# Expert slots of a two-layer block: the down product one slot later, the up weights in halves

## The chip, the cores and the metric

One NeuronCore of a Trainium2 chip runs the whole program. The metric is the device time of one execution in microseconds (us), as the median of several runs. PE is TensorE (PEld its weight loads), DVE VectorE, ACT ScalarE, POOL GpSimd, and SP the engine from whose queue most DMA transfers are issued. Each engine works through its own list of instructions in order and waits on semaphores of the others; while it waits, nothing behind the waiting instruction on that list can start.

## The reference

Two layers, each an attention block and a feed-forward block with gated residuals, on x of 4 x 512 x 512 in float32. The change lies in the first layer's feed-forward block, a mixture of 8 experts in which each token takes two, beside a shared expert. Cut to that:

```python
scores = softmax(xf @ gate_w)
_, sel = top_k(scores + expert_bias, 2)            # two experts for each of 2048 tokens
order = argsort(sel.reshape(-1), stable=True)      # rows sorted by expert
routed_in = xf[order // 2] * top_scores_sorted[:, None]
h = silu(ragged_dot(routed_in, w1, counts)) * ragged_dot(routed_in, w3, counts)
routed_out = ragged_dot(h, w2, counts)
out = silu(xf @ sw1) * (xf @ sw3) @ sw2
out = out.at[order // 2].add(routed_out)
```

An expert has 512 inputs, 448 hidden units and 512 outputs. The layer that follows is an attention with two sources of keys and a feed-forward block whose weights are rounded to three values.

## The kernel before

The parts of the block run one after the other, and each part prepares weights for a later one beside its own work. `moe` is the first layer's feed-forward block. It normalises the tokens, chooses the experts, scatters the scaled rows to a DRAM buffer of 39 slots of 128 rows each (`SLOTS`), runs the shared expert, and then loops over the slots. The rows of one slot belong to one expert, whose number is read from a small table by SP (`values_load`).

For each slot there are these steps.
- `load` reads the expert's number and sends for the up weights (`w13`, 1792 KB, two buffers that alternate). It is skipped on the chip where the expert is the one of two slots before.
- `load_rows` fetches the slot's 128 rows from ACT's queue, four slots ahead.
- `turn_in` (L861) transposes the rows in four 128 x 128 pieces on PE and copies them from PSUM to SBUF.
- `up` (L870) makes both up products in float32, `pu` and `pw`, over four chunks of the 512 inputs. ACT takes SiLU of `pu` (L874), DVE multiplies by `pw` (L875).
- `turn_hidden` (L881) transposes the hidden units in four pieces and copies them.
- `down` (L888) makes the down product. ACT scales it (L893) and its queue stores it in a second DRAM buffer.
- `load_down` (L855) sends for the down weights (`w2`, 896 KB, two buffers), skipped as `load` is.

The copies (`evac`, L120 on DVE and L122 on ACT) alternate between the two engines. SP's queue also carries two kinds of preparation in this loop. `split` holds the steps that split the second layer's weights in two halves of lower precision: a fetch (L1147), for some a scaling and a centring on DVE (L1137, L1115 to L1117), a cast on ACT (L1141), a subtraction on POOL (L1142) and a store (L1143) of 512 KB. There are 80 of them. `ternary` holds the steps that sum and then code the last block's weights: a fetch of 704 KB (L1890), DVE work (a sum, L1897, or three passes, L1920 to L1922), and for the coding a store (L1923).

The order of instructions on an engine isn't that of the source. A scheduler with a cost model chooses it from the dependences. Where `tc.keep_in_program_order` records an instruction (class `Ordered`), its order on the engine is the one in which the program emits it. In the slot loop before, nothing is recorded so. PE's list is up(s), hidden(s-1), in(s+1), down(s-1) for the middle slots, with some groups split or exchanged, and up(s), hidden(s), in(s+2), down(s) from slot 26 on.

After the loop the same function goes on to the keys and values of the second layer's context, 64 units of one product (`m_pk`) each, on PE in program order.

Of the kernel before, what the change touches and what calls it, by code (L numbers as in the profile page):

```python
# [22 lines left out]
P = 128  # L23
# [4 lines left out]
KC = D // P  # L28
# [5 lines left out]
E, HID, HC = 8, 448, 112  # L34
NHC = HID // HC
SLOTS = (2 * T + E * (P - 1)) // P
# [561 lines left out]
def moe(k, split, codes8, scratch, ffn):  # L598
# [11 lines left out]
    nc, tc, a = k.nc, k.tc, k.a  # L610
    with ExitStack() as ctx:
# [12 lines left out]
        w13 = [  # L624
            p1.tile([P, KC, 2, HID], F32, tag=f"m_w13_{j}", name=f"m_w13_{j}") for j in range(2)
        ]
# [38 lines left out]
        for b in range(B):  # L665
            k.layernorm([(xn[b][:, t, :], k.x[:, b * TB + t, :]) for t in range(TB)])
            for c in range(KC):
                pt = ps_m.tile([P, S], F32, tag="ps_m")
# [44 lines left out]
        def by_token(name):  # L713
            return p1.tile([P, NT], F32, name=name)
# [34 lines left out]
        pt = ps_m.tile([P, 2, NT, E], F32, tag="ps_m", name="r_counts")  # L749
# [41 lines left out]
        for r, hot in enumerate(hots):  # L791
# [8 lines left out]
            s = by_token(f"r_s{r}")  # L800
# [22 lines left out]
        got = {}  # L823

        def load(s):


            e = got["e", s] = nc.values_load(
                owners[:, s : s + 1], engines=(mybir.EngineType.SP,), min_val=0, max_val=E - 1,
                skip_runtime_bounds_check_because="it is at most E - 1 by construction",  # L830
            )
            got["new", s] = None if s < 2 else e != got["e", s - 2]
            nc.sync.dma_start(w13[s % 2], a["w13"][e], cond=got["new", s])

        def load_rows(s):
            work = p6.tile([P, 4, D], F32, tag="m_big", name=f"m_work{s}")
            rows = nc.scalar.dma_start(work[:, 0, :], rows_in[ts(s, P), :])
            for scatter in scatters:
                tc.add_manual_dep(
                    rows.ins, scatter.name,  # L840
                    mybir.DependencyInfo(mybir.DependencyClass.Sync, mybir.DependencyReason.DATA),
                    reason="any of them may write a row of the slot",
                )

            tc.add_manual_dep(
                rows.ins, silus[B * NHC - NHC - 1].name,
                mybir.DependencyInfo(
                    mybir.DependencyClass.NoSync, mybir.DependencyReason.SCHED_ONLY
                ),
                reason="order of ScalarE's queue",  # L850
            )
            got["work", s] = work

        def load_down(s):
            nc.sync.dma_start(w2[s % 2], a["w2"][got["e", s]], cond=got["new", s])  # L855

        def turn_in(s):
            work = got["work", s]
            pt = ps_m.tile([P, KC, P], F32, tag="ps_m")
            for c in range(KC):  # L860
                nc.tensor.transpose(pt[:, c, :], work[:, 0, ts(c, P)], k.ident)  # L861
            k.evac(work[:, 1, :].rearrange("p (c t) -> p c t", c=KC), pt)

        def up(s):
            work, w = got["work", s], w13[s % 2]
            pu = ps_h.tile([P, HID], F32, tag="ps_h")
            pw = ps_h.tile([P, HID], F32, tag="ps_h")
            for c in range(KC):
                for half, pp in enumerate((pu, pw)):
                    nc.tensor.matmul(  # L870
                        pp, lhsT=work[:, 1, ts(c, P)], rhs=w[:, c, half, :],
                        start=(c == 0), stop=(c == KC - 1),
                    )
            nc.scalar.activation(work[:, 2, 0:HID], pu, AF.Silu)  # L874
            nc.vector.tensor_tensor(work[:, 2, 0:HID], work[:, 2, 0:HID], pw, ALU.mult)  # L875

        def turn_hidden(s):
            work = got["work", s]
            pt = ps_m.tile([P, NHC, P], F32, tag="ps_m")
            for m in range(NHC):  # L880
                nc.tensor.transpose(pt[:HC, m, :], work[:, 2, ts(m, HC)], k.ident)  # L881
            k.evac(work[:HC, 3, :].rearrange("p (c t) -> p c t", c=NHC), pt[:HC])

        def down(s):
            work, w = got.pop(("work", s)), w2[s % 2]
            po = ps_o.tile([P, D], F32, tag="ps_o")
            for m in range(NHC):
                nc.tensor.matmul(  # L888
                    po, lhsT=work[:HC, 3, ts(m, P)], rhs=w[:, m, :],
                    start=(m == 0), stop=(m == NHC - 1),  # L890
                )
            y = p4.tile([P, D], F32, tag="m_row", name=f"m_y{s}")
            nc.scalar.activation(y, po, AF.Copy, scale=k.tg[:, 2:3])  # L893
            nc.scalar.dma_start(rows_out[ts(s, P), :], y)
# [3 lines left out]
        def load_weights(i):  # L898
            ws[i] = p6.tile([P, KC, 512], F32, tag="m_big", name=f"m_wx{i}")
            nc.sync.dma_start(ws[i], a["w_kvx"][i])  # L900

        def load_context(b):
            ctxT.append(p6.tile([P, KC, S], F32, tag="m_big", name=f"m_ctxT{b}"))
            nc.sync.dma_start(
                ctxT[b], a["ctxT"][:, ts(b, S)].rearrange("(c p) t -> p c t", p=P)
            )
# [4 lines left out]
        for s in range(2):  # L911
            load(s)
            load_down(s)
        turn_in(0)
        up(0)
        turn_in(1)
        for s in range(SLOTS):
            if s + 1 < SLOTS:
                up(s + 1)
            turn_hidden(s)  # L920
            if s + 2 < SLOTS:
                load(s + 2)
                turn_in(s + 2)
            down(s)
            if s + 2 < SLOTS:
                load_down(s + 2)
            if s + 4 < SLOTS:
                load_rows(s + 4)
            for _ in range(-(-len(split) // (SLOTS - s))):
                split.pop(0)(ps)  # L930
            if ternary:
                ternary.pop(0)()
            if s == SLOTS - 4:
                load_weights(0)
                load_context(0)
            elif s == SLOTS - 2:
                for c in range(KC):
                    centred(k, ws[0][:, c, 0:256], 2)


        kaff = p1.tile([P, 2], F32, name="kx_affine")
# [5 lines left out]
        VE, AE, GE, PE = (Ordered(tc, e) for e in (nc.vector, nc.scalar, nc.gpsimd, nc.tensor))  # L947
# [97 lines left out]
        got = {}  # L1045
# [54 lines left out]
        for c in range(KC):  # L1100
            m = 20 + 9 * c
# [8 lines left out]
def centred(k, w, heads):  # L1110

    nc = k.nc
    wv = w.rearrange("p (h d) -> p h d", d=D1)
    m = k.small.tile([P, heads], F32, tag="s_mean")
    nc.vector.tensor_reduce(m, wv, AX.X, ALU.add)  # L1115
    nc.vector.tensor_scalar(m, m, -1.0 / D1, None, ALU.mult)
    nc.vector.tensor_tensor(wv, wv, m[:, :, None].to_broadcast([P, heads, D1]), ALU.add)  # L1117
# [819 lines left out]
@with_exitstack  # L1937
def kernel(ctx: ExitStack, tc: tile.TileContext, a: dict, out: bass.AP):
    k = Kernel(ctx, tc, a, out)
    xattn_int8(k)  # L1940
    scratch, split = split_weights(k)
    with tc.tile_pool(name="codes", bufs=1) as pool:
        codes8 = Codes(k, pool)
        ffn = Ffn(k)
        first = moe(k, split, codes8, scratch, ffn)
        attend_and_feed(k, scratch, codes8, first, ffn)
# [85 lines left out]
```

## Time and profile before

| | us |
|---|---|
| median of 3 runs | 3576.08 (3575.98 to 3579.71) |
| the profiled execution | 3574.1 |
| its span | 3572.4 |
| slot stage, from its first transpose to the first m_pk | 869.14 to 1315.50 |

The profile comes from one execution, and a span in it begins with the first instruction. A row of the timeline gives start, duration, engine, line, what is written from what, and in brackets how long the engine stood idle before it and which instruction or transfer ended that. A matmul of float32 shows as two records. [...] L567 is the helper that records order, so many groups of later stages share that line.

### The profile page before, as it was taken

The numbers are of one execution on the slowest core, as the hardware profiler recorded it, in microseconds if no ns is written. First come the engines' busy times: TensorE is split into PE (matmuls) and PEld (weight loads), VectorE is DVE, ScalarE is ACT, GpSimd is POOL, SyncE is SP. The second block draws the span as 40 slices with busy tenths as digits, with TensorE's granted clock in tenths as the row PEclk, the third lists the DMA queues.
The fourth block names the chain that finished last, engine by engine and source line by source line (L and its number), as shares of the span: only waits on it lengthen the run. The fifth ranks groups of instructions, "written<-read, shape, count | busy, mean of one in ns | idle before, by whom it ended". The sixth has DMA issues, their size and how long they took to land.

```text
span 3572.4 us, 47015 instructions
## 1 busy us (share of the span) xinstructions
PE 3333.4 (93%) x15536; PEld 2190.3 (61%) x15552; DVE 2172.4 (61%) x4580; ACT 1544.1 (43%) x4456; POOL 1355.3 (38%) x1526
## 2 busy tenths in 40 slices
PE   6988987889999889989999999999999999999997
PEld 3544544534554444447777777776777777777775
DVE  6676767543133336525558766678766687676657
ACT  2544545111211223345554455554555554555543
POOL 1000000341000134624446654557545466544443
PEclk8999999899999999989999999999999999999998
DMA  5534441476354673552323233223332332333211
GB/s 183 156 98 130 121 101 41 167 254 234 104 198 151 225 257 128 177 174 72 115 98 107 101 115 110 95 99 108 109 125 92 118 107 77 128 105 111 83 60 36
DMA packets 223026, 452.86 MB, mean 127 GB/s; under 512 B 21440, under 2 KB 80320, under 8 KB 220224
## 3 DMA queue, kind: packets, MB, share of 16 engines
q1 hardware_dynamic: 206432, 412.62, 35.2%
q10 hardware_dynamic: 11232, 20.45, 1.7%
q0 software_dynamic: 5120, 16.78, 1.4%
q8 instruction: 125, 2.05, 0.2%
q14 instruction: 117, 0.96, 0.1%
HBM read 420.87 MB, written 116.98 MB: 151 GB/s over the span
## 4 chain that ended last, share of the span: by engine, by line
PE 73%; DVE 13%; DMA 4%; ACT 4%; POOL 3%; issue 3%; SPq 0%; DVEq 0%; POOLq 0%; ACTq 0%
PE ps_w L567 10%; PE pss L567 10%; PE ps_p L567 9%; PE ps_o L567 9%; PE ps_t L567 7%; PE m_pk L567 5%; PE po L888 3%; PE pu L870 3%; PE pw L870 3%; PE po L468 3%; PE pt L460 3%; DVE f_y L567 2%; PE pss L438 2%; PE pk L403 2%; PE pv L373 2%
## 5 line engine op out<-in xcount | busy, mean ns | idle before, releaser
L567 PEld LDWEIGHTS ps_w<-g_pT,g_v 128*128 128x128 f32 x2048 | 388.8, 191 | 299.7 <-issue 223.1
L567 ACT ACTIVATE g_p<-pss,nm 128x512 f32<-128x512 f32 x512 | 350.9, 685 | 479.7 <-DVE nm L567 436.4
L567 PE MATMUL ps_w<-g_pT,g_v 128*128 128x256 f32 x2048 | 530.4, 382 | 24.1 <-DVE f_y L567 13.7
L567 PE MATMUL pss<-g_kT,g_qT 128*128 128x512 f32 x1024 | 524.1, 594 | 0.9 <-ACT g_p L567 0.9
L567 POOL TENSOR_SCALAR g_p<-g_p,rs 128x512 f32<-128x512 f32 x512 | 368.4, 721 | 382.1 <-DVE rs L567 370.6
L567 DVE TENSOR_REDUCE nm<-pss 128x1 f32<-128x512 f32 x512 | 350.9, 685 | 102.7 <-PE pss L567 101.7
L567 PE MATMUL ps_t<-ident,g_p 128*128 128x128 f32 x2048 | 307.5, 273 | 0.0
L1142 POOL TENSOR_TENSOR hl<-raw,hl 128x512 fp32r<-128x512 f32 x80 | 102.0, 1282 | 519.2 <-ACT hl L1141 503.1
L567 POOL TENSOR_TENSOR g_rstd<-ss,neghalf 128x4 f32<-128x4 f32 (+1 forms) x192 | 185.0, 964 | 297.5 <-ACT ss L567 297.3
L567 PE MATMUL ps_p<-g_wq,g_xq 128*128 128x512 f32 x1024 | 282.3, 417 | 5.3 <-DMA g_wq<-s_q 4.9
L567 PE MATMUL ps_o<-g_wp,g_cq 128*128 128x512 f32 x1024 | 287.0, 423 | 0.0
L567 DVE COPY g_pT<-ps_t 128x512 f32<-128x512 f32 x244 | 167.1, 685 | 165.8 <-PE ps_t L567 165.4
L567 POOL TENSOR_TENSOR f_t<-f_y,f_c 128x512 f32<-128x512 bf16 (+1 forms) x180 | 206.6, 1148 | 155.4 <-DVE f_c L567 87.1
L567 PEld LDWEIGHTS ps_t<-ident,g_p 128*128 128x128 f32 x2048 | 243.8, 141 | 26.3 <-POOL g_p L567 1.1
L567 ACT COPY g_pT<-ps_t 128x512 f32<-128x512 f32 x268 | 156.1, 583 | 233.4 <-PE ps_t L567 233.4
L446 ACT ACTIVATE p<-pss,nm 128x512 f32<-128x512 f32 x256 | 175.3, 690 | 135.9 <-DVE nm L443 134.5
L567 PE MATMUL m_pk<-m_wx,m_ctxT 128*128 128x512 f32 x512 | 230.0, 592 | 0.0
L567 PEld LDWEIGHTS ps_o<-g_wp,g_cq 128*128 128x128 f32 x1024 | 196.7, 192 | 41.4
L567 PEld LDWEIGHTS ps_p<-g_wq,g_xq 128*128 128x128 f32 x1024 | 191.4, 190 | 48.9 <-issue 7.1
L443 DVE TENSOR_REDUCE nm<-pss 128x1 f32<-128x512 f32 x256 | 173.2, 687 | 70.7 <-PE pss L438 69.3
L567 ACT ACTIVATE junk<-ps_p 128x128 f32<-128x128 f32 x640 | 177.1, 277 | 68.5 <-PE ps_p L567 54.2
L567 DVE RECIPROCAL rs<-g_sm 128x1 f32<-128x1 f32 x512 | 82.5, 161 | 203.3 <-ACT g_p L567 201.4
(317 smaller groups left out, 6025.4 us busy)
## 6 DMA issues: line engine op xcount, KB each, us to landing
m_w<-in_w_dram SPq DMA_DIRECT2D x39, 1792.0 KB
g_wp<-s_proj SPq DMA_DIRECT2D x128, 512.0 KB
m_w<-in_w_dram SPq DMA_DIRECT2D x39, 896.0 KB
g_wq<-s_q SPq DMA_DIRECT2D x128, 256.0 KB
g_wq<-s_qx SPq DMA_DIRECT2D x128, 256.0 KB
st_k<-dhl_k SPq DMA_DIRECT2D x64, 256.0 KB
st_q<-dhl_q SPq DMA_DIRECT2D x64, 256.0 KB
s_proj<-hl SPq DMA_DIRECT2D x32, 512.0 KB
```

What stands on the lines that cost most here:

```text
L373: nc.tensor.matmul(pv, lhsT=ctxT[:, ic, ts(t, P)], rhs=wkvT[:, ic, D : 2 * D], start=(ic == 0), stop=(ic == KC - 1),)
L403: nc.tensor.matmul(pk, lhsT=wkvT[:, ic, ts(oc, P)], rhs=ctxT[:, ic, :], start=(ic == 0), stop=(ic == KC - 1),)
L438: nc.tensor.matmul(pss, lhsT=qk["q"][:, h, ts(qt, P)], rhs=qk["k"][:, h, :], start=True, stop=True,)
L443: nc.vector.tensor_reduce(nm, pss, AX.X, ALU.max, negate=True)
L446: nc.scalar.activation(p, pss, AF.Exp, bias=nm, accum_out=sums[:, qt, n : n + 1])
L460: nc.tensor.transpose(pt[:, c, :], p[:, ts(c, P)], k.ident)
L468: nc.tensor.matmul(po[ts(h, DH0)], lhsT=v[:, c, ts(oc * 4 + h, DH0)], rhs=pTs[h][:, c, :], start=(c == 0), stop=(c == TB - 1),)
L567: return lambda *args, **kw: self.tc.keep_in_program_order(call(*args, **kw))
L870: nc.tensor.matmul(pp, lhsT=work[:, 1, ts(c, P)], rhs=w[:, c, half, :], start=(c == 0), stop=(c == KC - 1),)
L888: nc.tensor.matmul(po, lhsT=work[:HC, 3, ts(m, P)], rhs=w[:, m, :], start=(m == 0), stop=(m == NHC - 1),)
L1142: nc.gpsimd.tensor_tensor(hl[:, 1, :], raw, hl[:, 0, :].bitcast(F32), ALU.subtract)
```

## The change

Four things change in the slot loop. PE's instructions are recorded in program order. The down product of a slot moves behind the up product of the slot after next in the emitted order: an iteration emits up(s+1), hidden(s), in(s+2), down(s-1), and the last down product follows the loop. The up weights come in two transfers of 896 KB, each with the same condition, and `load(s+3)` is emitted straight after `up(s+1)`, where `load(s+2)` stood after `turn_hidden(s)`. `load_down(s+1)` follows `down(s-1)`. The splitting steps are spread over the first 34 slots: 3 a slot for 12 slots and then 2, where they were 3 for two slots and then 2 to the end.

```diff
@@ load @@
-            nc.sync.dma_start(w13[s % 2], a["w13"][e], cond=got["new", s])
+            for c in (0, KC // 2):
+                some = slice(c, c + KC // 2)
+                nc.sync.dma_start(w13[s % 2][:, some], a["w13"][e][:, some], cond=got["new", s])
...
+        PE = Ordered(tc, nc.tensor)
+
         def turn_in(s):
...
-                nc.tensor.transpose(pt[:, c, :], work[:, 0, ts(c, P)], k.ident)
+                PE.transpose(pt[:, c, :], work[:, 0, ts(c, P)], k.ident)
...
@@ up, turn_hidden and down: nc.tensor becomes PE in the same way @@
...
         turn_in(0)
         up(0)
+        load(2)
         turn_in(1)
         for s in range(SLOTS):
+
             if s + 1 < SLOTS:
                 up(s + 1)
+            if s + 3 < SLOTS:
+                load(s + 3)
             turn_hidden(s)
             if s + 2 < SLOTS:
-                load(s + 2)
                 turn_in(s + 2)
-            down(s)
-            if s + 2 < SLOTS:
-                load_down(s + 2)
+            if s:
+                down(s - 1)
+                if s + 1 < SLOTS:
+                    load_down(s + 1)
             if s + 4 < SLOTS:
                 load_rows(s + 4)
-            for _ in range(-(-len(split) // (SLOTS - s))):
+            for _ in range(-(-len(split) // max(1, SLOTS - 5 - s))):
                 split.pop(0)(ps)
...
+        down(SLOTS - 1)
```

More of the change, by code (lines that the diff above doesn't have):

```diff
@@ L869, in up @@
                 for half, pp in enumerate((pu, pw)):
-                    nc.tensor.matmul(
+                    PE.matmul(
                         pp, lhsT=work[:, 1, ts(c, P)], rhs=w[:, c, half, :],
@@ L880, in turn_hidden @@
             for m in range(NHC):
-                nc.tensor.transpose(pt[:HC, m, :], work[:, 2, ts(m, HC)], k.ident)
+                PE.transpose(pt[:HC, m, :], work[:, 2, ts(m, HC)], k.ident)
             k.evac(work[:HC, 3, :].rearrange("p (c t) -> p c t", c=NHC), pt[:HC])
@@ L887, in down @@
             for m in range(NHC):
-                nc.tensor.matmul(
+                PE.matmul(
                     po, lhsT=work[:HC, 3, ts(m, P)], rhs=w[:, m, :],
```

## The prediction

> **What bounds the kernel now.** I read the page first, then the windows of the slot stage, then the waits of the weight-load side of TensorE (PEld), and last the order of time around three slots. The profiled execution took 3574.1 us (span 3572.4), 2.0 below the median of the three runs, 3576.1; I make the sum on its trace and subtract it from the median.
>
> ```profile
> PE 3333.4 (93%) x15536; PEld 2190.3 (61%) x15552; DVE 2172.4 (61%) x4580; ACT 1544.1 (43%) x4456; POOL 1355.3 (38%) x1526
> ```
>
> TensorE is the bound. Only time in which it idles, or runs slowly after idling, can be won. The change touches the 39 slots of the expert stage. There the windows (length, then busy time and count of PE, PEld, DVE, ACT, POOL, then clock, DMA share, GB/s) show a full PE first, and idle later:
>
> ```profile
> 1050.00:1100.00 50.00, 48.76 (x151) 25.03 (x150) 19.02 (x26) 8.80 (x15) 1.27 (x1) 1.00 0.58 191
> 1150.00:1200.00 50.00, 45.44 (x135) 22.33 (x134) 15.57 (x25) 12.39 (x21) 10.07 (x8) 1.00 0.63 222
> 1200.00:1250.00 50.00, 42.62 (x123) 20.58 (x122) 17.23 (x31) 10.44 (x18) 7.61 (x6) 0.97 0.65 226
> 1250.00:1320.00 70.00, 61.16 (x167) 28.82 (x166) 22.95 (x51) 16.68 (x29) 17.69 (x14) 0.98 0.70 248
> ```
>
> In the waits of PEld from 1130 to 1320 us (total, times, longest), the hidden transposes wait for DVE's product, the down product waits for ACT's copy, and few waits are for weights:
>
> ```profile
> PEld pt L881 <- DVE m_work L875: 21.5, 14, 2.7
> PEld po L888 <- ACT m_work L122: 8.3, 13, 1.6
> PEld pu L870 <- DMA m_w<-in_w_dram: 6.1, 3, 2.9
> ```
>
> The timeline of one late slot shows why. Its up product is followed at once by its own transposes and its own down product, so PE stands still twice:
>
> ```profile
> 1192.42 0.54 ACT L874 ACTIVATE m_work<-pu 128x448 f32<-128x448 f32 x1 [4.58 <-PE pu L870]
> ...
> 1193.24 0.62 DVE L875 TENSOR_TENSOR m_work<-m_work,pw 128x448 f32<-128x448 f32 x1 [9.33 <-PE pw L870]
> ...
> 1193.92 0.65 PE L881 MATMUL pt<-ident,m_work 128*112 128x128 f32 x4 [0.79 <-DVE m_work L875]
> ...
> 1195.24 3.70 PE L888 MATMUL po<-m_w,m_work 112*128 112x512 f32 x8 [0.24 <-ACT m_work L122]
> ```
>
> **The stage counted.** From the timeline of PE: an up product takes 6.02 us (16 records, start to start of what follows), a down product 3.43, a group of four transposes 0.44. A slot without waits is 6.02 + 3.43 + 2 x 0.44 = 10.33, and 39 slots are 402.9. The stage runs from the first transpose (869.14) to the first matmul of the next stage (m_pk, 1315.50): 446.4. So 43.5 us are lost. The starts of the up products say where. Slot 2 (887.37) to 24 (1124.21) is 10.77 a slot, a loss of 22 x 0.44 = 9.6. Slot 24 to 38 (1300.61) is 12.60 a slot; taking off one down product and one group of transposes that move into this stretch (3.87), 27.9 are lost. The rest, 6.0, lies at the two ends (2.0 of it is the last down product, which after a stand took 5.40). In the quiet late slots the period is 11.82, so 1.49 each is the two stands above; slots 33 and 34, whose experts are new, lose 2.2 and 4.3 more.
>
> **The change part by part.**
> *Down one slot later, PE in program order.* No instruction is added on PE, DVE or ACT. The instruction order of the changed kernel, built but not run, is up(s+1), hidden(s), in(s+2), down(s-1) for every slot. The hidden transposes have a whole up product (6.02) to cover DVE's product (0.62 and two hand-overs), the down product's copy is a slot old, and the down product (3.43) covers the copy of in(s+2) (0.69). DVE's order puts product and copy first and the splitting after them in nearly every slot. So the 43.5 can go. If the cover fails (a splitting step that waits for its DMA ahead of a copy on DVE), PE now cannot take other work, and the delay is paid whole.
>
> *The head keeps a loss.* Slots 0 to 2 have no down product between in and up. up0 waits 0.84 as now. up1 waits behind product (0.62) and copy (0.69) plus hand-overs, about 1.4. Before up2 DVE also has the sum over a w_dn piece (1.62 by its row): about 2.6. Together 4.9.
>
> *Up weights in halves, sent ahead.* The splits' stores wait on POOL in SP's queue, and whatever is behind them waits too. Here are the issues around the load of slot 33 in SP's timeline, and under them the PE row that waited for it:
>
> ```profile
> 1226.04 0.09 SPq L855 DMA_DIRECT2D m_w<-in_w_dram  x1
> 1226.24 0.84 SPq L1147 DMA_DIRECT2D raw<-in_w_q_dram  x2
> 1228.05 0.35 SPq L833 DMA_DIRECT2D m_w<-in_w_dram  x1
> ...
> 1236.45 1.02 PE L870 MATMUL pu<-m_w,m_work 128*128 128x448 f32 x2 [2.03 <-DMA m_w<-in_w_dram]
> ```
>
> Issues of 0.33 us and more move data, those of 0.1 are skipped; by that, slots 16, 17, 18, 33 and 34 fetch, and landing took 8.4 to 10.9 us. By the program, load(s+3) may go at the end of up(s+1), 2 x 4.31 + 6.02 = 14.6 before up(s+3): enough for 16 to 18. But in SP's new order the stores of a splitting step stand ahead of load 33, and two more between the halves of load 34. Load 33: product and copy (2.2 with hand-overs), 3.5 us of DVE, cast and two POOL operations (0.62 + 2 x 1.27) and the issues between put it about 9.7 after up31 ends. I let the first half land 5.5 later and the second 10, at 15.2 and 19.7; they are wanted at 14.6 and 17.6, so 0.6 and then about 1.8 is lost. Load 34: its second half goes out behind stores that wait for casts placed after slot 33's SiLU, some 17.7 after up32 ends; with 1 MB of stores before it it lands 7 later, at 25, and is wanted at 20 (up34 then begins at 17): 5 lost. The 896 KB down loads of 33 and 34, also behind stores, may miss by 1 each (896 KB took 6.27: 1239.83 to 1246.10). Together 9.4 stay, somewhat more than the 6.5 that these slots lose now.
>
> Each half adds one issue and its register work on SP, some 0.2 us, 39 times: nothing on the path while SP waits for others (by SP's waits L855 alone waits 151.5 us for PE). Two fetches issued together at 1166.88 were used by ACT at 1169.78 in two casts with no gap between (1.27 for both), so a second landing of the same queue costs next to nothing here. [...]
>
> *Splitting over 34 slots.* The same steps, none added; the last five slots are free of them. In slots 20 to 29 two steps meet one coding step of the feed-forward weights. There one turn of SP is: issue two fetches and the piece (1.3), landing 5.5 (1167.76 to 1173.30), three DVE passes 2.8, store 0.4: 10.0 against PE's 10.33, so it keeps up barely; I take 2 us of stalls (0 to 10). Another 2 for slots 14 to 18, where DVE has seven passes ahead of a product.
>
> *Sum.* 43.5 - 4.9 - 9.4 - 2 - 2 = 25.2 us. The next stage is PE without gaps (3.65 us a unit), so what comes early stays early. 3576.1 - 25 = 3551.
>
> **The rivals.**
> *Slower: SP's turn becomes the period.* Two such turns in the trace, from L855 to L855, took 14.24 and 15.62:
>
> ```profile
> 1136.88 0.09 SPq L855 DMA_DIRECT2D m_w<-in_w_dram  x1
> ...
> 1151.12 0.10 SPq L855 DMA_DIRECT2D m_w<-in_w_dram  x1
> ...
> 1161.80 2.85 SPq L1143 DMA_DIRECT2D s_kv<-hl  x2
> 1166.00 0.32 SPq L1923 DMA_DIRECT2D ffn_codes<-t_raw  x1
> 1166.74 0.09 SPq L855 DMA_DIRECT2D m_w<-in_w_dram  x1
> ```
>
> With half b of the up load behind the store of codes, PE would then wait each time. Ten slots at 14.93 cost 46 where I put 2: 3551 + 44 = 3595. It ends slower once a turn is over 10.33 + (25.2 + 2) / 10 = 13.05 in those ten. Against it: the issue at 1151.12 waited for a down product that ended at 1151.18 by its row, and the 15.62 had DVE idle 6.98 for PE's product first. These were PE's pace; the new DVE order takes that away.
>
> *Little gain.* PE keeps its order but is stopped about 0.35 a slot by late copies (39 x 0.35 = 13.7): gain 12, 3564. For it: the strict order; against: DVE is busy 15 to 20 of 50.
>
> *Nearly all.* The stores are earlier than I reckon, both loads are covered and SP keeps ahead: only the head and 3 us stay, 36 won, 3540. "Sent ahead" not doing what it says (loads still behind stores) is inside my forecast, not a rival.
>
> Order before the stage also shifts slightly (DVE held PE 6.41 at 855.20 in the shared part): plus or minus 4 on all.
>
> **How the numbers follow.** 0.2%, 7 us, is about what a measurement here can tell from no change. Forecast (gain 17 to 32): 0.56. Little gain (7 to 17): 0.17. Nearly all (over 32): 0.13. Within 7: 0.08, where two of the costs add up. Slower, almost all SP's turn: 0.06. So faster 0.86. The range 3540 to 3567 (gain 9 to 36) takes in the rivals' own values and the 4 us of the rule.
>
> **What would show it.** Right: PE's waits for the product and for the copy of the hidden units gone, a period near 10.3 in most slots, m_pk starting about 25 earlier with respect to the first transpose, waits for weights only at 33 and 34 (5 to 10 together). Wrong: up products of slots 20 to 29 waiting for a skipped load (SP behind), or copies of in(s+2) late in most slots; or the stage shorter but the next one starting later for want of ctxT or centred weights, both sent only after down product 34, 28 us before their use.

## The result, and the profile after

The changed kernel takes 3561.33 us (median of 5 runs, 3556.91 to 3564.90); the kernel before, run beside it, 3576.08 (5 runs, 3572.80 to 3579.71). The ratio is 0.996 with a 95% interval of 0.9949 to 0.9971: 14.8 us are won, between 10 and 18. I forecast 25 (3551) with a range of 3540 to 3567. The profiled execution took 3561.25 us (span 3559.5), 12.9 less span than before.

The page's first line, to be read against the one shown before, has TensorE still fullest by far, 10.1 us less busy for the same 15536 matmuls.

```profile
PE 3323.3 (93%) x15536; PEld 2189.1 (61%) x15552; DVE 2170.0 (61%) x4580; ACT 1544.1 (43%) x4456; POOL 1356.3 (38%) x1526
```

The windows of the slot stage (length, busy time and count of PE, PEld, DVE, ACT, POOL, then clock, DMA share, GB/s) show where the gain is, and where it stops:

```profile
1050.00:1100.00 50.00, 50.00 (x157) 26.11 (x156) 23.39 (x44) 12.43 (x21) 7.81 (x6) 1.00 0.62 207
1100.00:1150.00 50.00, 48.11 (x150) 24.46 (x149) 18.00 (x21) 12.73 (x22) 12.57 (x9) 1.00 0.68 241
1150.00:1200.00 50.00, 47.32 (x140) 23.91 (x139) 31.22 (x49) 11.99 (x20) 9.25 (x7) 0.97 0.61 207
1200.00:1250.00 50.00, 39.39 (x103) 19.19 (x102) 9.83 (x27) 9.57 (x17) 10.12 (x8) 0.87 0.69 242
1250.00:1320.00 70.00, 68.57 (x201) 33.96 (x200) 11.27 (x26) 18.40 (x45) 11.61 (x11) 1.00 0.61 214
```

From 1050 to 1100 us TensorE has no gap (48.76 of 50 busy before). From 1200 to 1250 it is worse than before: 39.39 busy against 42.62, at a clock of 0.87 against 0.97. TensorE's waits from 862 to 1320 us (total, times, longest) say what for:

```profile
PE pu L567 <- DMA m_w<-in_w_dram: 12.3, 6, 5.4
PE po L567 <- DMA m_w<-in_w_dram: 4.2, 4, 2.4
PE pu L567 <- issue: 2.1, 1, 2.1
PE pu L567 <- DVE m_work L120: 0.9, 1, 0.9
PE pu L567 <- ACT m_work L122: 0.7, 1, 0.7
```

The waits for the product (L879) and for the hidden copy are gone. In their place 16.5 us of waits for weights stand (5.8 before). ("Issue" is a wait for which the profile names no cause; it stands before up product 2.) In the sync queue, SP's, the lines of the changed kernel are L857 for the down loads, L835 for the up loads, L1156 for the fetches of splitting, L1152 for its stores and L1932 for the store of codes. Over the same stretch the stores of the split halves wait for GpSimd:

```profile
SPq L1152 <- POOL hl L1151: 128.3, 38, 11.5
```

Before they waited 153.8, so the waiting itself is not new; what is new is the pace that TensorE asks of the queue behind it. One turn of that queue, from one down load to the next (1103.35 to 1120.38), took 17.03 us:

```profile
1103.35 0.09 SPq L857 DMA_DIRECT2D m_w<-in_w_dram  x1
1103.49 0.83 SPq L1156 DMA_DIRECT2D raw<-in_w_proj_dram  x2
...
1116.12 2.20 SPq L1152 DMA_DIRECT2D s_proj<-hl  x2
1118.75 0.32 SPq L1932 DMA_DIRECT2D ffn_codes<-t_raw  x1
1119.85 0.09 SPq L835 DMA_DIRECT2D m_w<-in_w_dram  x1
1120.38 0.09 SPq L857 DMA_DIRECT2D m_w<-in_w_dram  x1
```

The two stores stand in the queue ahead of an up load's half and the next down load. What they wait for is in the rows of ScalarE and GpSimd:

```profile
1111.79 0.54 ACT L878 ACTIVATE m_work<-pu 128x448 f32<-128x448 f32 x1 [4.58 <-PE pu L567]
1112.98 0.59 ACT L122 COPY m_work<-pt 112x512 f32<-112x512 f32 x1 [0.65 <-PE pt L567]
1113.46 1.14 ACT L1150 CAST hl<-raw 128x512 fp32r<-128x512 f32 x2
...
1114.16 3.81 POOL L1151 TENSOR_TENSOR hl<-raw,hl 128x512 fp32r<-128x512 f32 x2 [12.56 <-ACT hl L1150]
```

The casts stand in ScalarE's order behind the SiLU of the slot, which itself waits for TensorE, and so the stores go out only when the next up product is over. From 1075.55 to 1226.86 the queue made 12 such turns in 151.3 us, 12.6 each, while TensorE needs 10.33. By the down load issued at 1203.54, whose buffer was free at 1186.19, it was 17.4 us behind. At slot 33, whose expert is new, TensorE pays:

```profile
1214.51 0.09 SPq L857 DMA_DIRECT2D m_w<-in_w_dram  x1
1214.70 1.59 SPq L1156 DMA_DIRECT2D raw<-in_w_kv_dram  x2
1217.16 1.12 SPq L835 DMA_DIRECT2D m_w<-in_w_dram  x2
```

```profile
1214.63 3.70 PE L567 MATMUL po<-m_w,m_work 112*128 112x512 f32 x8 [0.38 <-DMA m_w<-in_w_dram]
1223.69 1.83 PE L567 MATMUL pu<-m_w,m_work 128*128 128x448 f32 x2 [5.36 <-DMA m_w<-in_w_dram]
1225.31 1.70 PE L567 MATMUL pw<-m_w,m_work 128*128 128x448 f32 x2
...
1229.79 0.94 PE L567 MATMUL pu<-m_w,m_work 128*128 128x448 f32 x2
...
1245.15 1.86 PE L567 MATMUL pu<-m_w,m_work 128*128 128x448 f32 x2 [4.78 <-DMA m_w<-in_w_dram]
```

Both halves of load 33 were issued together, 14.6 us after up product 31 ended (1202.5), and landed in some 6.5. After the stand the first pairs of matmuls take 1.5 to 1.6 us, start to start, where a running TensorE takes 0.75 (its records, 0.92 long, overlap); the granted clock in the trace is 0.5 from 1223.00 to 1229.83. The second stand, at 1245.15, is the second half of load 34, which had been issued at 1237.89 behind two more stores.

### The profile page after: what moved, and what is told of

Read it like the earlier page. It is cut to its first block, busy times and chain, and to the rows that moved or that the text cites. A ratio compares the mean times of both kernels' runs of the same rounds, so it can differ in the third digit from the quotient of the medians.

```text
span 3559.5 us, 47228 instructions
## 1 busy us (share of the span) xinstructions
PE 3323.3 (93%) x15536; PEld 2189.1 (61%) x15552; DVE 2170.0 (61%) x4580; ACT 1544.1 (43%) x4456; POOL 1356.3 (38%) x1526
## 4 chain that ended last, share of the span: by engine, by line
PE 46%; DVE 7%; POOL 1%; ACT 1%; issue 1%; DVEq 0%; POOLq 0%; ACTq 0%
PE ps_w L567 10%; PE pss L567 10%; PE ps_p L567 9%; PE ps_o L567 9%; PE ps_t L567 8%; DVE f_y L567 2%; DVE t_work L567 1%; DVE nm L567 1%; DVE g_hn L567 1%; DVE f_e L567 1%; DVE g_pT L567 1%; DVE t_sm L567 0%; POOL g_rstd L567 0%; ACT junk L567 0%; DVE f_c L567 0%
## 5 line engine op out<-in xcount | busy, mean ns | idle before, releaser
L567 PEld LDWEIGHTS ps_p<-g_wq,g_xq 128*128 128x128 f32 x1024 | 191.0, 190 | 49.5 <-issue 6.4
```

The source lines that it names most:

```text
L567: return lambda *args, **kw: self.tc.keep_in_program_order(call(*args, **kw))
```

## The experiments

Theory 1: the sync queue falls behind because stores that wait for other engines stand ahead of the loads. Its rivals: the transfers themselves land late; the amount of splitting in the late slots is too much, whoever stores it; or all of the gain is TensorE's order and the rest is neutral. Ratios are to the kernel before, run on the same chip, with the 95% interval in brackets. "m_pk" is when the next stage's first matmul starts in the profiled execution: 1315.50 before, 1305.24 in the changed kernel.

**1. Of the change, only TensorE's order and the later down product.**

```diff
-            for c in (0, KC // 2):
-                some = slice(c, c + KC // 2)
-                nc.sync.dma_start(w13[s % 2][:, some], a["w13"][e][:, some], cond=got["new", s])
+            nc.sync.dma_start(w13[s % 2], a["w13"][e], cond=got["new", s])
...
-        load(2)
...
-            if s + 3 < SLOTS:
-                load(s + 3)
             turn_hidden(s)
             if s + 2 < SLOTS:
+                load(s + 2)
                 turn_in(s + 2)
...
-            for _ in range(-(-len(split) // max(1, SLOTS - 5 - s))):
+            for _ in range(-(-len(split) // (SLOTS - s))):
```

> Only PE's order and the down product one slot later are kept; up loads go whole and at their old place (load s+2 behind the hidden transposes of slot s), splitting is spread over 39 slots. Theory 1 (the sync queue falls behind because stores of the splitting and of the codes stand ahead of loads; it costs about 27 of the 31.5 us that the stage still loses): fewer splitting steps meet the codes' steps in one slot, so the queue's turn is nearer PE's 10.3 and the late loads are less late: 3545 to 3558, with slot starts 10.3 apart to slot 28. Theory 2 (the transfers themselves are slow to land; the queue's order matters little): whole loads issued later land later, new experts at 33 and 34 lose more: 3563 to 3570. Theory 3 (all of the gain is PE's order, the rest is neutral): 3561, as the changed kernel.

Measured: 3566.77, ratio 0.9981 [0.9974, 0.9989]; about half of the gain. The number is theory 2's, theory 1's is missed. But theory 2's mechanism does not show: the new experts at 33 and 34 stood 4.59 and 1.60, less than in the changed kernel (5.36 and 4.78). TensorE waited 10.7 us for weights and 13.3 for VectorE, spread over slots 18 to 38, and the sync queue still 147.2 for GpSimd at its stores: a thinner spread of splitting did not make that queue keep up. In the profiled execution m_pk started at 1302.71, no later than in the changed kernel, so this one profile does not show the difference between the medians. The order is worth some 7 us alone, and something else caps it.

**2. The stores of the halves issued by GpSimd, everywhere.**

```diff
-        nc.sync.dma_start(to, hl.bitcast(F32))
+        nc.gpsimd.dma_start(to, hl.bitcast(F32))
```

> The changed kernel with the stores of the split halves issued from GpSimd's queue, which makes the halves, so that the sync queue doesn't wait for GpSimd (before: 70 waits, 298.6 us between 600 and 1310). Theory 1: the down loads come at PE's pace, loads 33 and 34 go out within 3 us of the product that frees their buffer; the waits for weights from slot 24 on fall from 26 us to under 8: 3536 to 3545. Theory 2 (landing): those waits stay over 18 us: 3555 to 3563. Theory 3 (GpSimd becomes the late one, its stores holding up its own next halves and the kernels' other stages with stores of this kind): 3562 to 3580.

Measured: 3573.12, ratio 0.9999 [0.9990, 1.0007]: the whole gain was gone, and yet the slots ran as theory 1 says. The number is theory 3's, but not for its reason. From the first transposes (903.74) to m_pk (1317.58) the stage took 413.8 us where the changed kernel took 434.4; after the head nearly every slot period is 10.32 or 10.33, and there is no wait for weights at all. The stage started 33 us later. With the sync queue free, the order of instructions put more of the splitting into the shared part before the slots (44 of the 80 fetches of splitting stand ahead of slot 1's up load, 33 in the changed kernel), and there the passes of a split stand ahead of VectorE's product m_h. In the waits of TensorE and in VectorE's timeline of this run:

```profile
PE po L700 <- DVE m_h L696: 13.6, 2, 7.0
```

```profile
874.98 0.49 DVE L1146 TENSOR_SCALAR raw<-raw,pcol_sb 128x512 f32<-128x512 f32 x1 [10.46 <-DMA raw<-in_w_q_dram]
...
880.27 0.69 DVE L696 TENSOR_TENSOR m_h<-m_h,pw 112x512 f32<-112x512 f32 x1
```

VectorE stood 10.46 us for a fetch of splitting with m_h behind it. So the rival that the transfers are slow falls (the same loads, issued in time, were never late), but two explanations of the clean slots are left: the queue, or the smaller amount of late splitting.

**3. The changed kernel with whole up loads.**

```diff
-            for c in (0, KC // 2):
-                some = slice(c, c + KC // 2)
-                nc.sync.dma_start(w13[s % 2][:, some], a["w13"][e][:, some], cond=got["new", s])
+            nc.sync.dma_start(w13[s % 2], a["w13"][e], cond=got["new", s])
```

> The changed kernel with up weights loaded whole again, at the new early place. Theory 1: what counts is where the issue stands behind stores; if both halves stood together the time is the same, and where stores stood between the halves of load 34 (7.9 us apart) the whole load goes out at the first half's place: 0 to 6 us faster, 3555 to 3561. Theory 2 (landing; halves let PE begin on the first): 2 to 5 us slower, 3563 to 3566. [...]

Measured: 3561.34, ratio 0.9967 [0.9956, 0.9979], the changed kernel's time. It is the upper end of theory 1's range. Neither the 2 to 5 us that halves would save by theory 2 nor any cost of halves shows in the medians, though intervals of some 4 us to each side leave room for a part of either. In the profiled execution, the fastest of the seven (3555.01), the waits had moved: 7.3 us for weights, 11.1 for VectorE's copies of the next input.

**4. The changed kernel with the splitting over 39 slots.**

```diff
-            for _ in range(-(-len(split) // max(1, SLOTS - 5 - s))):
+            for _ in range(-(-len(split) // (SLOTS - s))):
```

> The changed kernel with the splitting over all 39 slots again. Theory 1: fewer splitting steps per slot up to slot 29, so a turn of the sync queue falls from 12.6 towards 11 and less lag is built up, but stores stand between loads to slot 38: 3550 to 3559. Rival (the last five slots free of splitting are what lets the stage end without loss): slots 34 to 38 lose 1.5 to 3 each in its place, 3562 to 3570.

Measured: 3563.01, ratio 0.9969 [0.9958, 0.9979]; its interval overlaps that of the changed kernel. It is the rival's number, and its mechanism shows in part: the slots that start at up products 35 and 36 took 17.33 and 14.28 us. But the slots before them lost so much less that m_pk started 11.6 us earlier (1293.66) than in the changed kernel. The next stage gave that back:

```profile
1315.37 0.69 PE L567 MATMUL m_pt<-ident,m_ring 128*128 128x128 f32 x2 [11.24 <-DVE m_ring L567]
```

```profile
1311.66 2.48 POOL L1151 TENSOR_TENSOR hl<-raw,hl 128x512 fp32r<-128x512 f32 x2 [7.62 <-ACT hl L1150]
1314.13 0.72 POOL L567 TENSOR_TENSOR m_rstd<-ss,neghalf 128x2 f32<-128x2 f32 x1
```

The last splits stand in GpSimd's order ahead of m_rstd, which the next stage's first m_ring needs. Time won in the slots is not kept by itself, as I had reckoned; what is queued for the end of the stage must be over too.

**5. Stores by GpSimd only from slot 16 on.** Up to there the order of the sync queue is the changed kernel's, and the late slots keep their two splits each.

```diff
+            k.store = nc.gpsimd if s >= 16 else nc.sync
             for _ in range(-(-len(split) // max(1, SLOTS - 5 - s))):
...
-        nc.sync.dma_start(to, hl.bitcast(F32))
+        k.store.dma_start(to, hl.bitcast(F32))
```

> The changed kernel with the stores of the split halves issued from GpSimd only in the steps that the program writes into slots 16 and later; the instruction order of the sync queue is the changed kernel's up to the load of slot 16, and slots 23 to 34 keep the same two splitting steps each, so that the amount of splitting there is unchanged. Theory 1 (loads wait behind stores that wait for GpSimd): waits for weights after slot 23, 21.9 us in the changed kernel, fall under 6, and the stage (434.4) to about 412: 3539 to 3547. Rival (the amount of splitting in the late slots, not the queue that stores it, delays the loads; in the run with all stores on GpSimd hardly any splitting was left there): 3557 to 3564, waits for weights over 15.

Measured: 3547.56, ratio 0.9924 [0.9911, 0.9938]. TensorE's waits for weights fell from 16.5 to 2.2 us, and m_pk came 13.9 earlier. From up product 23 to m_pk 26 fetches of splitting are issued, as in the changed kernel. So the amount of late splitting is not what delays the loads; the place of its stores is. It fell short of theory 1's range by a hair because 7.8 us of waits for VectorE's copy of the next input (L120) came in:

```profile
PE pu L567 <- DVE m_work L120: 7.8, 4, 3.9
PE pu L567 <- DMA m_w<-in_w_dram: 2.2, 3, 1.1
```

**6. Stores by GpSimd from slot 12 on** (the same edit with `s >= 12`).

> As before from slot 12 on instead of 16; some 12 splitting steps move from slots 16 to 27 to slots 4 to 15, where TensorE has no waits. Theory 1: as with 16, 0 to 3 us better since the codes' slots are lighter: 3537 to 3546. Rival (amount in the late slots; slots 28 to 34 keep two steps each): half of the way, 3550 to 3557.

Measured: 3539.24, ratio 0.9893 [0.9878, 0.9908], as theory 1 has it. No wait for weights is left, and the slice that was worst in the changed kernel (39.39 at a clock of 0.87) is:

```profile
1200.00:1250.00 50.00, 48.59 (x152) 25.08 (x152) 10.24 (x20) 13.68 (x24) 17.12 (x19) 1.00 0.88 308
```

**7. All stores on the sync queue, the splitting over by slot 20.**

```diff
-            for _ in range(-(-len(split) // max(1, SLOTS - 5 - s))):
+            for _ in range(-(-len(split) // max(1, 16 - s))):
```

> The changed kernel, all stores on the sync queue, with the splitting spread so that it ends by slot 20 or so (the codes' steps to slot 29 stay, slots 21 to 38 have no splitting). Rival (amount in the late slots): loads 33 and 34 stand behind nothing, the late waits go, 3540 to 3548. Theory 1 says the same of the late slots, but that slots 12 to 20 pay, four to six stores each standing between their loads, a turn of 15 to 20 us over eight slots: 30 to 60 lost there and 20 won later, 3570 to 3600.

Measured: 3611.27, ratio 1.0093 [1.0077, 1.0108]; slower than the kernel before by 33 us. From slot 21 on there is no loss, but the six periods from slot 14 to 20 average 24.9 us:

```profile
PE pu L567 <- DMA m_w<-in_w_dram: 40.7, 7, 11.1
PE po L567 <- DMA m_w<-in_w_dram: 13.2, 4, 8.1
PE t_pm L1916 <- DVE tot L1914: 12.0, 1, 12.0
```

This is my slower rival, brought about: once stores fill the queue, its turn is the period.

**8. Each store written one splitting step later, on the sync queue.**

```diff
+    held = []
...
-        nc.sync.dma_start(to, hl.bitcast(F32))
+        if held:
+            held.pop()()
+        held.append(partial(nc.sync.dma_start, to, hl.bitcast(F32)))
...
-    return s, steps
+    return s, steps + [lambda pool: held.pop()()]
```

> The changed kernel, all stores on the sync queue, but each store written one splitting step later, when GpSimd is long done; in the instruction order the store of one step of each pair now goes out at once and the other still stands behind its own cast of the same slot. Theory 1: about half of the sync queue's waits for GpSimd go and with them half of the late loss: 3548 to 3556. Rival (transfers or the amount of work): as the changed kernel, 3559 to 3563; if casts now wait for a buffer whose store is late, slower: 3565 to 3575.

Measured: 3560.09, ratio 0.9950 [0.9936, 0.9963], the changed kernel's time: theory 1's number missed. The queue's waits for GpSimd did fall (128.3 to 80.6), but the store that remains in each pair still waits for its cast, and loads 33 and 34 still stood behind it (4.2 to 5.4 each); another 8 came in at the first two up products. Half as many waiting stores is not half the delay.

**9. The kernel before, with stores by GpSimd from slot 12 and the splitting over 34 slots.**

```diff
+            k.store = nc.gpsimd if s >= 12 else nc.sync
-            for _ in range(-(-len(split) // (SLOTS - s))):
+            for _ in range(-(-len(split) // max(1, SLOTS - 5 - s))):
...
-        nc.sync.dma_start(to, hl.bitcast(F32))
+        k.store.dma_start(to, hl.bitcast(F32))
```

> The kernel before (down product behind its own transposes, whole up loads at their old place, PE's order free) with only the splitting over 34 slots and the stores of its halves on GpSimd from slot 12 on. If the queue's waits were what bounded the slots in the kernel before too (rival: the order of TensorE's work is worth nothing once the queue is free): 3540 to 3552. Theory 1 with the counted order (two stands a slot, 43.5 us lost, only the late loads' 6.5 and a part of late products belong to the queue): 3563 to 3573.

Measured: 3565.68, ratio 0.9969 [0.9957, 0.9981], within theory 1. With the queue free, the old order of TensorE still takes 10.83 us in a quiet slot, each down product standing 0.24 for ScalarE's copy of its own slot, and 0.5 lost a slot:

```profile
PE po L888 <- ACT m_work L122: 13.9, 33, 5.5
PE pu L870 <- DMA m_w<-in_w_dram: 5.0, 2, 2.5
```

**10 and 11. The queue free, and the halves, then also the early place, taken back.** Run 10 is run 6 with the edit of run 3. Run 11 also has load(s + 2) back behind the hidden transposes (the placing part of run 1's diff), with the splitting over 34 slots kept.

> The changed kernel with stores on GpSimd from slot 12 on and the up weights loaded whole at the early place. With the queue free, a whole load sent 14.6 us before its use lands in 8.4 to 10.9: halves are worth nothing, 3537 to 3543 (with halves: 3539.2). Rival (halves let TensorE start on the first): up products of the five new experts wait 1 to 3 each, 3543 to 3552.

> As the last, with the whole up loads at their old place (load s+2 behind the hidden transposes of slot s), so that of the change only TensorE's order, the later down product and the splitting over 34 slots remain, with the stores on GpSimd from slot 12. If the early place matters once the queue is free: the new experts' loads land 2 to 5 late, 3545 to 3555. If not (the load waits for the same up product either way and nothing stands ahead of it): 3536 to 3543.

Measured: 3537.85, ratio 0.9890 [0.9874, 0.9905], and 3536.75, ratio 0.9892 [0.9877, 0.9907]. Neither the halves nor the early place shows a gain once no store that waits stands ahead of a load. Run 11 is the fastest of all, about 39 us under the kernel before. Its waits and its down loads in the late slots:

```profile
PE pu L567 <- ACT m_work L122: 1.5, 2, 0.8
PE pu L567 <- DMA m_w<-in_w_dram: 1.5, 1, 1.5
PE pu L567 <- DVE m_work L120: 1.1, 1, 1.1
```

```profile
1210.78 0.07 SPq L855 DMA_DIRECT2D m_w<-in_w_dram  x1
...
1221.11 0.35 SPq L855 DMA_DIRECT2D m_w<-in_w_dram  x1
...
1231.43 0.33 SPq L855 DMA_DIRECT2D m_w<-in_w_dram  x1
```

Down loads go out 10.32 us apart: TensorE's own pace, also for the two that move data. By then no splitting is left in this run (its last two fetches go out at 1183.25), so its late slots are lighter than those of run 10, which has two fetches in each slot from 27 to 35 and waits 0.7 us for weights.

**12. Run 1 with the stores by GpSimd from slot 12** (splitting over 39 slots).

> TensorE's order and the later down product alone (whole up loads at their old place, splitting over 39 slots), with the stores on GpSimd from slot 12 on. It differs from the run of the order alone (3566.8, ratio 0.9981) in the stores' engine only. Theory 1 (of the change only TensorE's order is worth anything once the queue is free): 3534 to 3542, as with 34 slots (3536.8). Rival (the spread over 34 slots is needed, the last slots' splitting delays the end of the stage or the start of the next): 3543 to 3555.

Measured: 3548.99, ratio 0.9920 [0.9906, 0.9933]; to run 1, from which its program differs in the stores' engine alone, it is 22 us by the ratios (18 by the medians, on two chips). The 12 to run 11 are in the rival's range, but are not lost at the end: from slot 19 on nothing is. They stand in the head (up0 4.97 for ScalarE, up1 6.07 for VectorE) and at slot 18's load (4.96, after which the up product took 8.54 for 6.1). With the queue free, the spread over 34 slots matters through the place that the instruction order gives to the early splits, not through quiet last slots. That is read from the two traces and was not tested further.

The main runs side by side (waits in the slot stage, us):

| kernel | median | TensorE's waits for weights | sync queue's stores waiting for GpSimd | its fetches of splitting waiting for GpSimd | m_pk |
|---|---|---|---|---|---|
| before | 3576.1 | 5.8 | 153.8 | none | 1315.5 |
| changed | 3561.3 | 16.5 | 128.3 | none | 1305.2 |
| 5: GpSimd from 16 | 3547.6 | 2.2 | 6.0 | 49.5 | 1291.4 |
| 6: GpSimd from 12 | 3539.2 | none | 2.7 | 22.9 | 1287.9 |
| 7: all by slot 20 | 3611.3 | 53.9 | 126.1 | none | 1359.2 |
| 9: before, GpSimd from 12 | 3565.7 | 5.0 | 0.7 | 76.7 | 1312.2 |
| 11: order, GpSimd from 12 | 3536.8 | 1.5 | 0.7 | 84.3 | 1279.4 |

Two things limit what the table shows. First, "free" does not mean that nothing in the queue waits. With the stores gone, its fetches wait for the buffers that GpSimd's subtraction reads:

```profile
SPq L1153 <- POOL hl L1148: 84.3, 39, 5.5
```

That is run 11, the fastest. What counts is that the turn stays within TensorE's period, as it does there (10.32 from one down load to the next). Second, moving the stores let the order bring splitting forward. From up product 23 to m_pk 31 of the 80 fetches are issued in the kernel before, 26 in the changed kernel and in run 5, 22 in run 10, 20 in run 6, and 14 or 15 in runs 9, 11 and 12. So run 5 is the one that moves the stores and leaves the late work as it was. What the others won beyond it belongs to the queue and to lighter late slots together, and was not taken apart.

By the ratios, TensorE's order alone (run 1) wins 7 us and the stores by GpSimd alone (run 9) 11, but both (run 11) 39; with the splitting over 39 slots, as in run 1, both win 29 (run 12). With the old order TensorE stood for its own neighbours; with the new order it reached the pace at which the queue could not follow.

## Why the prediction was right, and which term was off

Direction and range held: 14.8 us were won of 25 forecast. But the gain lies below the forecast's own band (17 to 32), in the one from 7 to 17 to which I gave 0.17; that the range held owes much to its width, which took in the rivals. In the profiled execution the stage lost 31.5 us over its clean 402.9 where I had left 18.3.

- *Down one slot later, order of TensorE: right.* Slot 3 to 24 ran at 10.35 us a slot (10.77 from slot 2 to 24 before). A slot's clean 10.33 is now what most slots take.
- *Head: right.* 4.45 lost, 4.9 forecast.
- *Slots 14 to 18: less than I put.* 0.3 lost in all of slots 3 to 24, where I had set 2.
- *Heavy slots: nearly right in size, wrong in the ground given.* 3.2 lost in slots 24 to 28, 2 forecast. But the ground, "one turn of SP is 10.0", failed: turns took 12.6 on average. I had counted the fetch, VectorE's passes and a store, and had left out that the casts stand behind a SiLU that waits for TensorE, and that GpSimd's pair took 3.8 us there, not 2.5. In these slots the loads are skipped ones and had slack, so most of the delay did not show; it was handed on. What showed was the sign of being wrong that I had named: up products 24 to 27 stood 0.15 to 1.16 us for the second half of a skipped load.
- *The loads of 33 and 34: the mis-sized term.* I left 9.4 there; slots 29 to 37 lost 23.5. The landings were as reckoned (7.3 for load 34's second half, 7 forecast). The issues were not: I put load 33 at 9.7 after its buffer was free and it went out at 14.6; 17.7 for the second half of 34, and it was 24.7. The difference is, as far as the issues tell, the lag brought along from slots 18 to 28, which I took to be nought. And I charged only the stands: the half rate after them cost a further 3.1 at slot 33, some 2.7 at 34, and 1.8 in a down product (1180.96, which took 5.23 for 3.43). The two down loads of 33 and 34 lost the 2 that I gave them.
- *The halves: next to nothing, as read from the trace, is what the medians show.* No run shows the 4 us "of the rule" that the range took in: run 3 beside the changed kernel and run 10 beside run 6 show differences of 0.0 and 1.4, inside their intervals, which are too wide to exclude a smaller cost.
- *The rivals.* The slower one, in which SP's turn becomes the period, was half at work: its turn of 12.6 is just under the 13.05 from which I had it decide. My argument against it (that the long turns were TensorE's pace, which the new order would take away) failed: the turns stayed long. Run 7 is what it looks like in full. Little gain (12) came nearest in number, but not by its mechanism, late copies: the changed kernel has 1.6 us of those.
- *"What comes early stays early"* held for the changed kernel (m_pk 10.3 earlier, 2.6 more won later) but run 4 shows that it need not.

That loads 33 and 34 stand "behind stores" was in the forecast. What was missing is that this queue kept its lateness from turn to turn: an excess of some 2.3 us a turn (12.6 for 10.33), far from any real load, had grown to 17.4 us by 1203.54 and was paid at the first real load, which went out 14.6 us after its buffer was free. That the lag behind waiting stores is the cause is shown by run 5 above all, which moves the stores, keeps the late work, and has 2.2 us of waits for weights in place of 16.5. Run 2, with no wait for weights in its slots, shows that the transfers are not slow, and run 7 that a queue full of stores sets the period (24.9 us on average from slot 14 to 20). How the some 7 us between run 1 and the changed kernel are shared among the halves, the early place and the spread was not settled; runs 3 and 4 each take back one of them and lie within a few us of the changed kernel.

## What to carry to other kernels

Before giving the bounding engine a tighter order, compare the turn of every in-order queue that feeds it with the new period, counting what each entry waits for on other engines: where the turn is longer, a large part of the gain is lost there (the changed kernel won 15 us, run 11 won 39). Let the engine that makes a result issue its store, so that the queue of loads keeps its turn within the period (10.32 in run 11). Do it only where the work cannot drift ahead: moved everywhere (run 2), the same edit took 20.6 us off the stage, which started 33 us later.

## What the hardware showed that I had not expected

*A stand could cost more than itself, and whether it did went with when it fell.* Taken over the runs, an up product that stood only before its first matmul, for up to 1.8 us, then took its usual 6.1. After stands of 2.0 to 3.4 us it took either 6.1 or about 7.8 (2.25 in run 10: 7.82; 2.36 in run 1: 7.79; 2.35 in run 5: 6.12; 3.34 in run 1: 6.12), and after 3.5 or more always 7.7 or longer. The granted clock tells the two apart. In the traces of the kernel before and the changed kernel it is 1.00 or 0.50 and nothing else, and within each trace all its changes lie on one grid of 3.41 us. In run 1 the grid cut the stand of 3.34 us (1256.27 to 1259.61) in two, while nearly all of the stand of 2.36 (1281.39 to 1283.75) fell in one stretch of the grid. These windows, set on the grid, give TensorE's busy time and, as the first number behind the count, its clock:

```profile
1254.30:1257.71 3.41, 1.96 (x5) 1.00 0.68 207
1257.71:1261.12 3.41, 1.51 (x4) 1.00 0.00 0
1261.13:1264.54 3.41, 3.41 (x10) 1.00 0.71 287
...
1281.61:1285.02 3.41, 1.27 (x4) 1.00 0.99 344
1285.02:1288.43 3.41, 3.41 (x6) 0.50 1.02 360
```

From 862 to 1320 us the traces of the kernel before and the changed kernel have 259 such stretches at full clock. All 4 in which TensorE was busy for less than 0.40 were followed by one at half clock, and none of the 254 with 0.50 or more was; in between, the one with 0.46 was (before, 1307.78), and run 1's with 0.44 (1257.71 above) was not. The share is that of this stage's matmuls, with their ends modelled. A stand shorter than a stretch was enough for the half rate (1.5 for 0.75 us a pair): 2.25 us in run 10, 2.36 in run 1.

*VectorE's passes and GpSimd's pairs were slower together.* In the slots with both, a pass of VectorE over 128x1408 that began while GpSimd's subtraction ran took 1.4 to 2.0 us for 0.9 (14 passes in the kernel before and the changed kernel). In the changed kernel, where such passes covered two thirds of it or more, GpSimd's pair took 3.44 to 3.89 us for 2.49. The first pass below began before GpSimd's (1114.16) and kept its time:

```profile
1114.02 0.94 DVE L1929 TENSOR_SCALAR t_raw<-t_raw,sc_w_gu 128x1408 f32<-128x1408 f32 x1
1115.00 1.84 DVE L1930 TENSOR_SCALAR t_raw<-t_raw 128x1408 f32<-128x1408 f32 x1
1116.88 1.84 DVE L1931 TENSOR_SCALAR t_raw<-t_raw 128x1408 fp8e4<-128x1408 f32 x1
...
1129.03 0.89 DVE L1930 TENSOR_SCALAR t_raw<-t_raw 128x1408 f32<-128x1408 f32 x1
```

Why was not shown. A store that GpSimd issues takes time of its own: in run 2 it took 0.6 us on GpSimd and its bytes landed after 3.8 to 5.1 (medians by kind). ScalarE's casts waited 89 us in all for the buffers of these stores, but TensorE stood only 1.4 us for a cast.
